# Filler products of layer 1, first half: four column tiles or the whole width of TensorE's array

## The chip, the cores and the metric

The kernel runs on one core of one Trainium2 chip. The metric is the device time of one execution in microseconds. Every measured program is run several times, and the median is compared.

## What is computed

Two cross-attention layers follow each other, for a batch of 4, all in float32. In layer 0, `x` (4, 1024, 512) goes through a layer norm and attends to `ctx_768` (4, 1024, 384) with 16 heads of 64. In layer 1, the result goes through an RMS norm and attends to the same context with 16 heads of 32. There the queries and keys are rotated by position and brought to unit length first. The core of layer 1, cut to what matters here:

```
q = (xn @ wq).reshape(B, T, 16, 32)
kv = (ctx @ wkv).reshape(B, T, 2, 16, 32);  k, v = kv[:, :, 0], kv[:, :, 1]
q, k = rotate(q, cos, sin), rotate(k, cos, sin)
q, k = q / norm(q), k / norm(k)
attn = softmax(einsum('bqhd,bkhd->bhqk', q, k) * sqrt(32))
out = x + einsum('bhqk,bkhd->bqhd', attn, v).reshape(B, T, 512) @ wout
```

## The kernel before, in words

The batch entries are worked through one after the other (loop at L739). For each, layer 0 runs over 8 pairs of heads (L746), and layer 1 over two halves of 8 heads each (L849). The change concerns layer 1.

**A step of layer 1.** One half is 32 steps: 4 blocks of 256 queries, 2 groups of 4 heads, and 4 pairs of key tiles (L885, L886). A step (`Attention1.step`, L590) puts this on the engines, in this order:

- *Scores*, L597: 8 matmuls, `s`, each with 32 rows and 128 columns of the array. Four heads lie in four row tiles of the array side by side, each 32x128. They fill two PSUM tiles of two banks each.
- Two exponentials on ScalarE, L607, from those PSUM tiles into `e`.
- *Products of the step before*, L636: 8 matmuls, `av`, each with 128 rows and 32 columns, so that four heads lie in four column tiles, each 128x32. After the last pair of key tiles, 8 more, L647, with a matrix of ones: the sums under the softmax. Those read `both`, which VectorE has added up.
- *Filler*, L611: `self.u.fill(us)` takes units from a queue and issues them until their assumed cost covers the share of this step.
- Additions on VectorE of the exponentials, L613 and L617, for the sums.

**The filler.** Whatever the attention of this half doesn't need yet is cut into units, each a function with a cost in microseconds written out by hand (`Units`, L54). `weave` (L94) sets them in order. In half 0 of layer 1 these are the projections of the remaining queries (`q[1]` to `q[3]`, `q1`), keys (`k1[2]`, `k1[3]`) and values (`vs`), 92 matmul units in all, each a product of a 128x128 block with 256 columns of weights (L490, L562). Between them lie 12 places with transposes by TensorE through an identity matrix: ten with 4 for a rotated query or key block (L519), and two, with 12 and 4, for the normalized rows (L253). In half 1 they are the projections of the next batch entry and the output product of this one.

**How wide a filler matmul is.** All filler products go through `matmul` (L153). It splits one product into `which["cols"]` instructions, each with a slice of the columns of the stationary matrix, so that each takes one column tile of the array:

```
w = P // which["cols"]
for j in range(which["cols"]):
    rr = slice(j * w, (j + 1) * w)
    nc.tensor.matmul(o[rr], lhsT[:, rr], rhs, start=start, stop=stop)
```

In layer 0, `cols` is 2 (L122, L899). L837 sets it to 4 for all of layer 1, the shape of `av`. The transposes don't go through it: they are always 128x128.

**After a projection.** When a query or key projection is complete, `rotate` (L494) follows. ScalarE squares it (L497), VectorE does five operations (L499 to L504), GpSimd does three (L506, L175, L510), and then TensorE transposes the result (L519) and ScalarE copies it out (L524). `post` (L163) issues this chain at once in layer 1. VectorE also divides (L654, L655) after each block.

**Order and due times.** The order on each engine is the order in which the program issues, since `manual_schedule` is on (L117). `marks` (L864) says up to which unit the queue must be worked off before steps 8, 16 and 24. PSUM has two score tiles of two banks (L120). One further bank is held by `av` in layer 1, and three banks rotate among the fillers (`bank`, L124).

Each float32 matmul stands in the trace as two pairs of records, LDWEIGHTS and MATMUL; a transpose stands as one. The text calls one MATMUL record of all tiles that work side by side a *pass*.

Of the kernel before, what the change touches and what calls it, by code (L numbers as in the profile page):

```python
# [93 lines left out]
def weave(chains, lag):  # L94

    res = []
    for i in range(len(chains) + lag):
        if i < len(chains):
            res += chains[i][0]
        if 0 < i <= len(chains):  # L100
            res += chains[i - 1][1]
        if i >= lag:
            res += chains[i - lag][2]
    return res
# [3 lines left out]
def xattn_kernel(ctx: ExitStack, tc: tile.TileContext, a: dict, out: bass.AP):  # L108
# [13 lines left out]
    which = {"n": 0, "from": 0, "cols": 2}  # L122
# [16 lines left out]
    cols = const.tile([P, 3, NQ], F32, name="cols")  # L139
# [152 lines left out]
    def add_units(xt, lhs, w, name, cs, then=None):  # L292

        n = len(cs)

        def one(t, i, pp=[None]):
            if i == 0:
                pp[0] = bank(f"{name}_{t}")
            matmul(pp[0], lhs(cs[i])[:, t * P : (t + 1) * P], w(cs[i]), i == 0, i == n - 1)
            if i == n - 1:  # L300
                nc.vector.tensor_add(xt[t], xt[t], pp[0])  # L301
                if then is not None:
                    then(t)

        return [[(0.86, lambda t=t, i=i: one(t, i)) for i in range(n)] for t in range(NT)]
# [250 lines left out]
    def value_chains(v, wv, ct, name):  # L556
        def one(t0, i, k, st={}):
            if i == 0 and k == 0:
                st["pp"] = bank(f"{name}_{t0}")
            t = t0 + i  # L560
            lhsT = ct[t // 4][:, k, (t % 4) * P : (t % 4 + 1) * P]
            matmul(st["pp"][:, i * FH : (i + 1) * FH], lhsT, wv[:, k, :], k == 0, k == NC_ - 1)  # L562
            if i == TH - 1 and k == NC_ - 1:
                pv = st["pp"].rearrange("p (t g d) -> p g t d", t=TH, g=2)
                for g in range(2):
                    nc.scalar.copy(v[g][:, t0 : t0 + TH, :], pv[:, g])

        return [
            ([(0.44, lambda t0=t0, i=i, k=k: one(t0, i, k)) for i in range(TH) for k in range(NC_)], [], [])
            for t0 in range(0, NT, TH)  # L570
        ]
# [89 lines left out]
    def wo_load(src, i, name):  # L661
        w = sb.tile([P, 2, DQ], F32, tag="wo", bufs=2, name=name)
        nc.sync.dma_start(w, src[i * 2 * P : (i + 1) * 2 * P, :].rearrange("(n p) m -> p n m", p=P))
        return w

    def flat(lists):
        return [u for lst in lists for u in lst]
# [71 lines left out]
    for b in range(B):  # L739
# [94 lines left out]
        work.add(norms[0]["turn"] + q[0][0] + k1[1][0] + k1[0][2] + flat(outs[4:]) + q[0][2])  # L834
        work.drain()

        which["from"], which["cols"] = 1, 4  # L837
        att1 = Attention1(b, work)
        o = [
            sb.tile([P, S], F32, tag="vals", bufs=4, name=f"o1_{b}_{g}") if g < 2 else None  # L840
# [7 lines left out]

        for half in range(2):  # L849
            n = 0  # L850
            if half == 0:
                vs = value_chains(att1.v1, wv1, ct, f"pv1_{b}_1")
                first = [q[1], (norms[1]["stats"], [], []), vs[0], (norms[1]["apply"], [], k1[1][2]), k1[2]]
                rest = [(norms[1]["turn"] + q[2][0], [], q[2][2]), k1[3], q[3], q1[0], vs[1], q1[1], q1[2]]
                rest += [q1[3], vs[2], vs[3]]
                chains = first + rest
                work.add(weave(chains, 2))
                def mark(c):

                    i = chains.index(c)  # L860
                    return sum(len(x[0]) for x in chains[: i + 3]) + sum(len(x[2]) for x in chains[: i + 1])

                base = work.done
                marks = {8: base + mark(q[1]), 16: base + mark(rest[0]), 24: base + mark(q[3])}  # L864
            else:
                for g in range(2, 4):
                    o[g] = sb.tile([P, S], F32, tag="vals", bufs=4, name=f"o1_{b}_{g}")
                wo1 = [wo_load(a["wout"], i, f"wo1_{b}_{i}") for i in range(2)]
                adds = add_units(xt, lambda n: o[n], lambda n: wo1[0][:, n % 2, :], f"po1_{b}_0", (0, 1))
                if b + 1 < B:  # L870
                    st, order = prepare_units(b + 1)
                    work.add(order(adds))
                else:
                    work.add(flat(adds))
            blocks = [(qb, g) for qb in range(S // WQ) for g in range(2)]
            final = b == B - 1 and half == 1
            if final:
                blocks.sort(key=lambda block: block[1])
                adds = [
                    add_units(  # L880
                        xt, lambda n: o[n], lambda n: wo1[1][:, n % 2, :], f"po1_{b}_{i}", (i,), store if i == 3 else None
                    )
                    for i in (2, 3)
                ]
            for qb, g in blocks:  # L885
                for kk in range(NT // 2):  # L886
                    if half == 0 and n in marks:
                        work.until(marks[n])
                    if final and n == 18:
                        work.add(flat(adds[0]))  # L890
                    if final and n in (22, 26, 30):
                        work.add(flat(adds[1][(n - 22) // 2 : (n - 18) // 2]))
                    att1.step(half, g, qb, kk, kT, qT, v, o[2 * half :], work.total() / (32 - n))
                    n += 1
            work.drain()
            kT, qT, v = kT1, qT1, att1.v1
# [48 lines left out]
```

## Time and profile before

| | |
|---|---|
| median of 3 runs | 2974.82 us (2970.41 to 2974.82) |
| the profiled execution, its own time | 2969.33 us |
| its span in the profile | 2967.1 us |
| granted TensorE clock | 0.999 |
| TensorE busy (matmul) | 2905.4 us, 98% |
| VectorE busy | 2230.9 us, 75% |
| ScalarE busy | 1430.4 us, 48% |
| half 0 of layer 1, the four batch entries | 508.3 to 638.8, 1242.7 to 1373.1, 1976.5 to 2106.9, 2711.8 to 2843.9 us |

The profile is of one execution; its own time is 5.5 us below the median of the runs. All times in the views are microseconds from the start of the span. A matmul's busy time overlaps with that of its neighbours, since they are pipelined and their ends are modelled. So distances from start to start are used below.

### The profile page before, as it was taken

The page shows a single profiled execution, that of the slowest core. Times are in us where ns is not written, and L with a number is a line of the kernel's source. Part 1 is how long each engine was busy: PE and PEld are TensorE (multiplying, and loading weights), DVE is VectorE, ACT ScalarE, POOL GpSimd, SP SyncE. Part 2 cuts the span into 40 slices and gives each one's busy share as a digit, 9 for nine tenths or more (in the row PEclk, how much of TensorE's full clock was granted, in tenths as well). Part 3 has the DMA queues.
Part 4 walks back from the last instruction along what each step waited for, and adds up shares of the span by engine and source line. Part 5 has one row for each costly group of instructions (what it writes and reads, how often), then busy time and mean ns, then how long its engine had stood idle before and what let it go on. Part 6 is the DMA issues. An engine that isn't in the chain of part 4 may idle for free.

```text
span 2967.1 us, 66793 instructions
## 1 busy us (share of the span) xinstructions
PE 2905.4 (98%) x27880; PEld 1454.7 (49%) x27880; DVE 2230.9 (75%) x2824; ACT 1430.4 (48%) x2265; POOL 417.2 (14%) x392
## 2 busy tenths in 40 slices
PE   8999999999999999999999999999999999999998
PEld 4544445555544444555544444455455444445544
DVE  4777795877777779587777777958767777785777
ACT  3444443666544444466644444446664443444664
POOL 0010022420000002232000000224100000023310
PEclk9999999999999999999999999999999999999999
DMA  5787674010388867301048777730105978772000
GB/s 146 173 198 181 158 178 111 21 35 25 80 205 192 186 159 179 91 22 35 25 100 214 182 182 171 165 79 22 35 25 120 211 177 186 166 171 62 2 2 30
DMA packets 177549, 348.88 MB, mean 118 GB/s; under 512 B 37600, under 2 KB 93152, under 8 KB 177248
## 3 DMA queue, kind: packets, MB, share of 16 engines
q1 hardware_dynamic: 175056, 343.43, 48.9%
q8 instruction: 220, 3.60, 0.5%
q10 hardware_dynamic: 2192, 1.19, 0.1%
q14 instruction: 81, 0.66, 0.1%
HBM read 67.64 MB, written 8.39 MB: 26 GB/s over the span
## 4 chain that ended last, share of the span: by engine, by line
PE 85%; DVE 7%; DMA 2%; ACT 2%; SPq 1%; issue 1%; POOL 1%; DVEq 0%; ACTq 0%
PE s L372 16%; PE av L449 14%; PE po L158 11%; PE pv L158 8%; PE s L597 7%; PE pqT L158 7%; PE av L636 6%; PE pkT L158 5%; PE q_p L158 3%; PE av L647 2%; PE k_p L158 2%; DVE both L613 2%; PE rT L440 1%; DVE both L617 1%; SPq L407 1%
## 5 line engine op out<-in xcount | busy, mean ns | idle before, releaser
L396 ACT ACTIVATE e<-s,m 128x1024 f32<-128x1024 f32 x512 | 566.1, 1110 | 666.3 <-DVE m L395 625.8
L395 DVE TENSOR_REDUCE m<-s 128x1 f32<-128x1024 f32 x512 | 602.7, 1219 | 314.0 <-PE s L372 314.0
L607 ACT ACTIVATE e<-s 128x1024 f32<-128x1024 f32 x512 | 496.7, 1022 | 312.4 <-PE s L597 297.3
L401 DVE STREAM_TRANSPOSE e<-e 128x1024 f32<-128x1024 f32 x512 | 606.7, 1223 | 47.6 <-ACT e L396 44.7
L372 PE MATMUL s<-qk 64*128 64x512 f32 x2048 | 521.3, 615 | 5.4 <-ACT e L396 4.7
L449 PE MATMUL av<-eT,v 128*64 128x256 f32 x4096 | 465.2, 380 | 7.3 <-DMA eT<-e 3.7
L613 DVE TENSOR_TENSOR both<-e 128x512 f32<-128x512 f32 x512 | 342.1, 700 | 125.0 <-ACT e L607 89.8
L449 PEld LDWEIGHTS av<-eT,v 128*64 128x64 f32 x4096 | 295.1, 137 | 186.2 <-issue 48.4
L372 PEld LDWEIGHTS s<-qk 64*128 64x128 f32 x2048 | 182.4, 186 | 269.2 <-issue 193.3
L597 PE MATMUL s<-q,k 32*128 32x256 f32 x4096 | 305.1, 401 | 5.8 <-ACT q L524 2.7
L597 PEld LDWEIGHTS s<-q,k 32*128 32x128 f32 x4096 | 191.2, 184 | 149.2 <-ACT e L607 72.0
L158 PE MATMUL po<-wo,vals 128*64 128x512 f32 x1024 | 239.7, 599 | 3.0 <-ACT v L130 3.0
L158 PE MATMUL pqT<-hT,w 128*64 128x512 f32 (+1 forms) x1216 | 241.4, 598 | 0.7 <-ACT hT L255 0.7
L441 ACT COPY vals<-rT 128x256 f32<-128x256 f32 x128 | 47.8, 373 | 323.7 <-PE rT L440 323.7
L301 DVE TENSOR_TENSOR x<-x,po 128x512 f32<-128x512 f32 x200 | 134.0, 678 | 83.0 <-PE po L158 82.7
L158 PEld LDWEIGHTS pv<-w,cT 128*64 128x64 f32 (+1 forms) x3648 | 168.5, 128 | 34.3 <-issue 31.2
L158 PE MATMUL pv<-w,cT 128*64 128x128 f32 (+1 forms) x3648 | 183.4, 274 | 0.0
L158 PE MATMUL pkT<-cT,w 128*64 128x512 f32 (+1 forms) x912 | 182.0, 601 | 0.9 <-ACT cT L130 0.9
L617 DVE TENSOR_TENSOR both<-both 128x1024 f32<-128x1024 f32 x128 | 159.7, 1248 | 4.4
L636 PE MATMUL av<-e,v 128*32 128x256 f32 x2048 | 137.1, 385 | 0.0
L636 PE MATMUL av<-e,rest 128*32 128x256 f32 x2048 | 137.0, 385 | 0.0
L158 PE MATMUL q_p<-wq,hT 128*32 128x256 f32 (+1 forms) x1920 | 131.2, 380 | 0.0
(461 smaller groups left out, 2482.0 us busy)
## 6 DMA issues: line engine op xcount, KB each, us to landing
eT<-e SPq DMA_DIRECT2D x2048, 128.0 KB, 2.4
xr<-in_x_dram SPq DMA_DIRECT2D x32, 256.0 KB, 4.1
x<-in_x_dram SPq DMA_DIRECT2D x32, 256.0 KB, 3.7
wo<-in_Wo_dram SPq DMA_DIRECT2D x16, 512.0 KB, 4.2
out_dram<-x SPq DMA_DIRECT2D x32, 256.0 KB, 2.6
w<-in_Wq_dram SPq DMA_DIRECT2D x31, 256.0 KB, 4.0
c<-in_ctx_dram SPq DMA_DIRECT2D x32, 192.0 KB, 3.8
wkv<-in_wkv_dram SPq DMA_DIRECT2D x16, 384.0 KB, 3.2
```

The source lines that it names most:

```text
L158: nc.tensor.matmul(o[rr], lhsT[:, rr], rhs, start=start, stop=stop)
L301: nc.vector.tensor_add(xt[t], xt[t], pp[0])
L372: nc.tensor.matmul(sc[j][:, kb * 512 : (kb + 1) * 512], pr["qT"][r[j], i * P : (i + 1) * P], pr["kT"][r[j], kb * 512 : (kb + 1) * 512], st ...
L395: nc.vector.tensor_reduce(m[:, j : j + 1], sc[j], AX.X, ALU.max, negate=True)
L396: nc.scalar.activation(e[j], sc[j].rearrange("p (g s) -> p g s", g=4), AF.Exp, bias=m[:, j : j + 1], accum_out=l[:, j : j + 1])
L401: nc.vector.transpose(e[j], e[j])
L449: nc.tensor.matmul(av[r[j], :W].rearrange("p (t a i) -> p t a i", t=BQ, a=4), pr["v"][:, k, r[j]], eT[:, j, :, :, k * 32 : (k + 1) * 32], ...
L597: nc.tensor.matmul(sc[j // 2][:, j % 2, c, :], kT[rr, g, k * P : (k + 1) * P], qT[rr, g, qb * WQ : (qb + 1) * WQ], start=True, stop=True,)
L607: nc.scalar.activation(e, sc[u], AF.Exp, scale=float(np.sqrt(np.float32(HD1))))
L613: nc.vector.tensor_add(self.both[:, kk, 2 * u : 2 * u + 2, :], es[u][:, :, 0, :], es[u][:, :, 1, :])
L617: nc.vector.tensor_add(self.both[:, 0], self.both[:, 0], self.both[:, kk])
L636: nc.tensor.matmul(self.av[rr, 0, :], v[g][:, 2 * kk + c, rr], es[j // 2][:, j % 2, c, :], start=first and c == 0, stop=end and c == 1,)
```

## The change

`cols` is no longer set once for layer 1, but at the start of each half: 1 in half 0, 4 in half 1. With 1, `matmul` issues one instruction with all 128 columns in place of four with 32 each. The 92 filler products of half 0 are then 92 instructions for each batch entry, in place of 368. What is computed, the order of the units, the steps into which they fall, and every other instruction stay the same.

```
-        which["from"], which["cols"] = 1, 4
+        which["from"] = 1
         att1 = Attention1(b, work)
...
         for half in range(2):
             n = 0
+            which["cols"] = (1, 4)[half]
             if half == 0:
```

More of the change, by code (lines that the diff above doesn't have):

```diff
@@ L835, in xattn_kernel @@
         work.drain()
-        which["from"], which["cols"] = 1, 4
+        which["from"] = 1
         att1 = Attention1(b, work)
@@ L850, in xattn_kernel @@
             n = 0
+            which["cols"] = (1, 4)[half]
             if half == 0:
```

## The prediction

> **What bounds the kernel now.** I read the busy shares first, then the chain that ended last, then the stage that changes.
>
> ```profile
> PE 2905.4 (98%) x27880; PEld 1454.7 (49%) x27880; DVE 2230.9 (75%) x2824; ACT 1430.4 (48%) x2265; POOL 417.2 (14%) x392
> ...
> PE 85%; DVE 7%; DMA 2%; ACT 2%; SPq 1%; issue 1%; POOL 1%; DVEq 0%; ACTq 0%
> ```
>
> TensorE is busy for 98% and makes 85% of the chain. By stretches (columns: busy us and instructions of PE, PEld, DVE, ACT, POOL), half 0 and then half 1 of layer 1 of the first batch entry:
>
> ```profile
> 508.30:638.80 130.50, 124.41 (x1916) 69.38 (x1916) 102.99 (x143) 82.33 (x109) 47.53 (x30) 1.00 0.06 17
> 638.80:770.50 131.70, 131.42 (x1979) 69.68 (x1978) 92.73 (x129) 82.55 (x100) 3.75 (x4) 1.00 0.12 35
> ```
>
> Half 0 is the one stage where PE stands idle for some microseconds (6.1 of 130.5), and DVE is at 79%. So extra PE time there is paid, except what falls into those waits. The steps themselves (start, length, records; PE timeline):
>
> ```profile
> 508.31 1.15 PE L597 MATMUL s<-q,k 32*128 32x256 f32 x16 [0.68 <-ACT q L524]
> 509.39 1.93 PE L158 MATMUL q_p<-wq,hT 128*32 128x256 f32 x32
> 511.25 1.36 PE L597 MATMUL s<-q,k 32*128 32x256 f32 x16
> 512.55 1.07 PE L636 MATMUL av<-e,v 128*32 128x256 f32 x16
> 513.44 1.48 PE L158 MATMUL q_p<-wq,hT 128*32 128x256 f32 x24
> 514.85 1.15 PE L597 MATMUL s<-q,k 32*128 32x256 f32 x16
> ...
> 526.33 0.66 PE L519 MATMUL q_t<-ident,rot 128*128 128x128 f32 x4 [0.57 <-POOL rot L510]
> 526.92 1.07 PE L158 MATMUL k_p<-wkv,cT 128*32 128x256 f32 x16
> 527.92 1.15 PE L597 MATMUL s<-q,k 32*128 32x256 f32 x16
> ```
>
> A pass of four tiles with 256 columns takes 216 ns from start to start (single records in the trace). Two column tiles: 216 too; transposes: 109. From these and the line starts I take the price of each change of shape, as an exit part (paid by the last pass of the old shape) and an entry part (paid by the first of the new):
> - `av` after `s`: 512.55 to 513.44 = 889 ns, 4 passes are 864: entry into 128x32 costs 24.
> - filler after `av`, then `s`: 513.44 to 514.85 = 1409, 6 passes are 1296: nothing at entry, exit from 128x32 costs 114.
> - transposes, then filler: 526.33 to 526.92 = 587 against 4 x 109 = 436: 56 at entry, 94 at exit.
> - `s`, then `av`: 1075 (508.31 to 509.39 rounds it), against 864: 104 at entry of 32x128, 108 at exit.
>
> These numbers give back every undisturbed run of PE in the half within 2 ns.
>
> [...] The trace agrees: 94 to 114 ns at each change, none between `av` and a filler of the same shape. [...] The entry costs agree: 24 (128x32), 51 (128x64, layer 0), 104 (32x128). Transposes, 56, are faster than that. [...] The trace agrees for 128x128 transposes: 109 a pass, load included.
>
> **The change, part by part.** The built order of PE shows the same steps, with 92 filler instructions in place of 368 per batch entry.
>
> *Passes.* 92 units x 2 passes stay 184 passes. No full-width float32 product is in this trace. I take 216 ns, as with two and four tiles[...]. Gain or loss zero; bounds 196 (below) and 216 + 105 = 321 if the load were not hidden.
>
> *Changes of shape.* Full width enters at about 104 (by the columns; between 0[...] and 104; transposes show 56) and exits at 94 as a single tile (transposes). Between transposes and full-width products the shape is the same: I take 0; the upper bound is a full change, 94 + 104 or 94 + 56. The 32 steps of a half 0 fall into these kinds:
> - 19 with filler only after `av` or the sums: a new change, 114 + 104, less 20 at the exit: +198.
> - 4 with transposes, then filler: change saved, 94 + 24, and 20 at the exit: -138.
> - 5 with filler, then transposes: +218, less 114 + 56: +48.
> - 3 with transposes between filler: +218 less (114 + 56) less (94 + 24) less 20: -90.
> - step 0, with no `av`: 104 for 24, 94 for 114: +60.
>
> Sum: 19 x 198 - 4 x 138 + 5 x 48 - 3 x 90 + 60 = 3240 ns per batch entry, 13.0 us in all.
>
> *What the waits take back.* The prices above sum to 120.3 us for a half 0 that takes 130.5, so PE waits about 10 us in it for something else (6.1 shows as idle; in the rest some of the tiles wait while others run). If that hangs on an event before the delay, the wait shrinks by the delay. The largest:
>
> ```profile
> 622.63 0.61 PE L647 MATMUL av<-both,ones 128*32 128x256 f32 x8
> 625.47 1.01 PE L647 MATMUL av<-both,ones 128*32 128x256 f32 x6 [2.22 <-DVE both L613]
> ```
>
> DVE has been busy without a break since
>
> ```profile
> 610.57 0.69 DVE L499 TENSOR_TENSOR rot<-q_p,cos 128x512 f32<-128x512 f32 x1 [2.65 <-ACT rot L497]
> ```
>
> which ACT's L497 (609.94) released, and that the end of the filler of step 24. So all delay from steps 25 to 27 vanishes here. I go through the half with the delay D in ns:
> - step 0: +60, gone in step 1, whose scores wait 218 for an exponential. Step 1: D = 198.
> - steps 2 and 3: their 396 vanish in step 4 (waits of 734 in its scores and 635 before its transposes; ACT, DVE and GpSimd run in one chain from the scores of step 2). Rest of step 4, -138: 60.
> - step 5: 258; step 6's transposes wait 1.67 on DVE, in the same chain: 198. Steps 7, 8: 258.
> - step 9's filler ends at 258 + 218 = 476 and starts the next DVE chain (549.16); the sums of step 12 wait 2.36 on it: 476, after its transposes 338.
> - step 13: 536; filler of step 14: 754, starting the chain of 570.26; sums of step 16: 754, then 952. Step 17: 862, 18: 1060, 19: 1108.
> - sums of step 20, wait 0.17, chain from the exponentials of step 17: 952, then 1150. Steps 21 to 23: 1456.
> - sums of step 24, wait 0.17, chain from step 22: 1348, its filler ends at 1566; sums of step 28: 1566, then 1764. Steps 29 to 31: 2058.
>
> So 2.06 us of the 3.24 remain; half 1 has PE waits of 0.6 us only, and passes it on. The last entry's half 1 waits more (15 us), but for ScalarE and VectorE that follow its own scores, which come later by the same D. 4 x 2.06 = 8.2 us. On the profiled execution, 2969.33 + 8.2 = 2977.6; the median of runs stands 5.5 higher, so I state 2974.82 + 8.2 = 2983.0. Covers that could go: the order on ACT, DVE, POOL and the queues does not change, and no DMA waits for a filler of this half closely (share 0.06).
>
> **Rivals.** About 0.2% (6 us) is what a measurement can tell from no change.
> - *No relief from the waits* (D is carried whole): 13.0, 2987.8. For: anchors such as ACT's L497 at 609.94 wait for the filler's end themselves. Against: DVE's unbroken runs before the waits.
> - *Transposes and products don't share a mode*: 7 exits from transposes into products at 198, and 8 the other way at 150, are 2.6 us per entry; 8.2 + 10.3 = 18.5, less some relief: about 2990. For: a transpose has one pass and a faster load. Against: same rows and columns.
> - [...]entry of 0 in place of 104 makes a plain step +94; the same walk ends at 0.7 us per entry: 2.8, 2977.6, no visible change. With 56 it ends at 1.4: 5.6. Against: all three loads above show at entry.
> - *Full-width loads are not hidden at all*: 184 x 105 ns = 19.3 us per entry, 77 in all, 3060. Against: the transposes' 109.
> - *Faster*: the four tiles of a pass start 7 ns apart, 20 in all, and 196 lie from the last to the next. If a single tile saved those 20, the passes of the filler would take 196: 184 x 20 = 3.7 us per entry against 2.06, or 6.5 us faster, 2968.3. It decides from a pass below 205 ns on (2.06 us / 184 = 11 ns). Against: transposes and 32-column tiles with 128 columns both take 109, so the stagger costs nothing.
>
> **How the numbers follow.** Chances: my forecast 0.49 (its own range 2979 to 2988), no relief 0.15, no shared mode 0.12, [...] 0.13, loads exposed 0.04, faster 0.07. Predicted: 2983. The range, 2976 to 2996, takes in the hidden load below, and no relief and the unshared mode above; it leaves out the exposed loads and the faster case. Slower by over 0.2%: 0.42 of my 0.49, and 0.31: 0.73. Within: 0.07 and 0.13: 0.20. Faster: 0.07.
>
> **What would show it.** In the profile after: a filler pass of 216; 1409 + 104 - 20 for 3 units after `av` (about 1493), with `av` before it at 864 + 24 + 114 = 1002 in place of 889; transposes to filler at 109, not 203; half 0 at 132.5 us in place of 130.5, half 1 unchanged; the PE waits for `both` (3.8 us) shorter. Wrong if `av` stays at 889, or if transposes still pay at each end.

## The result, and the profile after

The changed kernel takes 2979.14 us (median of 13 runs, 2976.32 to 2985.89) against 2970.41 us for the kernel before (13 runs in all with the three shown first, 2966.13 to 2974.97). The ratio is 1.003, with a 95% interval from 1.0022 to 1.0038: slower by 8.7 us, and by 6.5 to 11.3 within the interval. The forecast was 8.2. The profiled execution took 2979.14 us, with a span of 2976.8.

On the page after, matmul busy time is up by 11.1 us, with 2208 records fewer:

```profile
PE 2916.5 (98%) x25672; PEld 1492.5 (50%) x25672; DVE 2231.1 (75%) x2824; ACT 1432.6 (48%) x2265; POOL 416.8 (14%) x392
```

Busy times by stretch after, half 0 and half 1 of the first batch entry, columns as before:

```profile
508.90:641.30 132.40, 126.86 (x1360) 78.74 (x1360) 103.03 (x143) 82.35 (x109) 47.53 (x30) 1.00 0.05 16
641.30:773.30 132.00, 131.71 (x1979) 69.73 (x1978) 92.82 (x129) 82.81 (x101) 3.74 (x4) 1.00 0.12 35
```

Half 0 went from 130.5 to 132.4 us. Half 1 hardly moved. In half 0, DVE, ACT and POOL do the same work in the same time as before. The same steps on PE as in the prediction, now after the change:

```profile
508.93 1.15 PE L597 MATMUL s<-q,k 32*128 32x256 f32 x16 [0.68 <-ACT q L524]
510.00 1.99 PE L158 MATMUL q_p<-wq,hT 128*128 128x256 f32 x8
511.93 1.30 PE L597 MATMUL s<-q,k 32*128 32x256 f32 x16
513.16 1.07 PE L636 MATMUL av<-e,v 128*32 128x256 f32 x16
514.16 1.56 PE L158 MATMUL q_p<-wq,hT 128*128 128x256 f32 x6
515.65 1.15 PE L597 MATMUL s<-q,k 32*128 32x256 f32 x16
...
527.14 0.66 PE L519 MATMUL q_t<-ident,rot 128*128 128x128 f32 x4 [0.57 <-POOL rot L510]
527.64 1.03 PE L158 MATMUL k_p<-wkv,cT 128*128 128x256 f32 x4
528.60 1.15 PE L597 MATMUL s<-q,k 32*128 32x256 f32 x16
```

`av` to filler now takes 513.16 to 514.16, 1.00 us, where it was 0.89: the exit from four column tiles is paid there. The 6 passes of the filler take 514.16 to 515.65, 1.49 us, where it was 1.41. Before, they paid nothing at entry and 0.11 at the exit from four column tiles; now they pay a load of 128 columns at entry (0.10) and an exit of 0.09. The four transposes take 0.50 to the next product (527.14 to 527.64), where it was 0.59: nothing is paid at their exit. These nine lines hold both signs that the prediction asked for.

Measured exactly, from the start of the first score matmul to that of the next half, the four halves 0 take 130.46, 130.46, 130.46 and 132.09 us before, and 132.41 each after. The 132.09 holds 1.6 us more in steps 28 and 29 than the other three. The trace shows why: the granted TensorE clock (the third figure from the end) falls to about half there, for 3.4 us:

```profile
2830.00:2833.00 3.00, 3.00 (x28) 1.36 (x24) 2.85 (x4) 0.59 (x1) 2.92 (x2) 0.52 0.03 5
```

Such a stretch stands in other runs at other places, also where nothing was changed: after, from 1650.3 to 1653.7 us, in layer 0, at a clock of 0.50. Each half 0 in the traces of this document that is 1.4 to 1.6 us longer than its siblings holds one, and no other half 0 does. So the undisturbed 130.46 is what to compare with: the delay is 1.95 us per half 0, 7.8 in all. The halves 1 add 0.24, 0.30, -0.10 and 0.02. That makes 8.2 in this pair of profiles, beside 8.7 us between the medians. The distance of the two spans (9.7 us) is made up otherwise: it lacks the 1.6 us that the profile before lost to the clock, and holds 3.1 more in layer 0, which the change doesn't touch. From half 1 of one entry to half 0 of the next, layer 0 takes 472.2, 471.6 and 472.2 us before, and 473.1, 474.4 and 471.0 after; the 474.4 holds that stretch at half clock, and what else scatters there was not traced.

### The profile page after: what moved, and what is told of

Same layout as the page of the kernel before. It is cut to its first block, busy times and chain, and to the rows that moved or that the text cites. A ratio compares the mean times of both kernels' runs of the same rounds, so it can differ in the third digit from the quotient of the medians.

```text
span 2976.8 us, 62377 instructions
## 1 busy us (share of the span) xinstructions
PE 2916.5 (98%) x25672; PEld 1492.5 (50%) x25672; DVE 2231.1 (75%) x2824; ACT 1432.6 (48%) x2265; POOL 416.8 (14%) x392
## 4 chain that ended last, share of the span: by engine, by line
PE 83%; DVE 9%; DMA 2%; ACT 2%; SPq 1%; issue 1%; POOL 1%; DVEq 0%; ACTq 0%
PE s L372 15%; PE av L449 13%; PE po L158 10%; PE pv L158 8%; PE s L597 7%; PE pqT L158 7%; PE av L636 6%; PE pkT L158 5%; PE q_p L158 4%; PE av L647 2%; DVE both L613 2%; PE k_p L158 1%; PE rT L440 1%; DVE e L401 1%; DVE m L395 1%
## 5 line engine op out<-in xcount | busy, mean ns | idle before, releaser
L613 DVE TENSOR_TENSOR both<-e 128x512 f32<-128x512 f32 x512 | 342.7, 700 | 125.7 <-ACT e L607 90.0
L617 DVE TENSOR_TENSOR both<-both 128x1024 f32<-128x1024 f32 x128 | 159.7, 1248 | 4.4
L158 PE MATMUL q_p<-wq,hT 128*128 128x256 f32 (+1 forms) x576 | 132.6, 393 | 0.0
```

Source lines behind the costliest of these rows:

```text
L613: nc.vector.tensor_add(self.both[:, kk, 2 * u : 2 * u + 2, :], es[u][:, :, 0, :], es[u][:, :, 1, :])
L617: nc.vector.tensor_add(self.both[:, 0], self.both[:, 0], self.both[:, kk])
```

## The experiments

The theory was that of the prediction: filler after a product pays a change of the array's shape, transposes ahead of filler save one, and later waits in half 0, most of them on VectorE, take back a third of the sum. Rivals: the extra time belongs to half 0 rather than to the shape; the price grows with the width of an instruction; nothing is taken back, and the price was over-estimated.

### Full width in half 1 alone

The edit is against the changed kernel, as is the next one.

```
-            which["cols"] = (1, 4)[half]
+            which["cols"] = (4, 1)[half]
```

> The filler is full-width in half 1 alone, four tiles in half 0. If the delay is the price of changes of shape (218 ns after each product, 20 back at the exit, 118 saved after transposes), half 1 of the first three batch entries, which has 24 plain steps, 4 with transposes ahead of the filler and 3 with transposes behind it, gets longer by 24 x 198 - 4 x 138 + 3 x 48 + 336 = 4.7 us each, nearly all of it paid since TensorE waits for only 0.6 us there; the last entry's, with 9 steps without filler and 15 us of waits, by 2 to 4.7. In all 16 to 19 us slower than the kernel before. If instead the extra time in half 0 comes from something of that half (its VectorE chains, its transposes), half 1 gets longer by less than 2 us each.

Measured: 2990.49 us (4 runs), ratio 1.0068 (1.0054 to 1.0082), 20 us slower (16 to 24), where 16 to 19 were expected. Halves 0 stand at 130.4 again, but for one with a stretch at half clock. By stretches, half 1 of the first entry and of the last:

```profile
638.60:775.40 136.80, 136.53 (x1425) 73.69 (x1424) 92.92 (x129) 82.66 (x100) 3.74 (x4) 1.00 0.11 33
...
2858.20:2977.00 118.80, 113.22 (x1245) 53.71 (x1244) 92.65 (x121) 67.83 (x75) 0.00 (x0) 1.00 0.04 15
```

The four are longer by 5.1, 5.0, 4.4 and 3.3 us (the first 136.8 against 131.7, the last 119.2 against 115.8, from start to start), 17.8 in all; the rest up to 20 was not traced. By the prices of the prediction, passes and changes of shape in the first come to 131.06 us before and 135.74 here, the 4.68 expected. Of the other 0.4, 0.2 lie in the passes of 128 columns, which take 112 ns in place of 109, and 0.2 in waits. So the extra time is not something of half 0; that it goes by the shape and not by the width, the next two runs show. Where few transposes stand next to the filler and PE waits little, the same edit costs two and a half times as much (5.1 us against 1.95).

### Two column tiles in half 0

```
-            which["cols"] = (1, 4)[half]
+            which["cols"] = (2, 4)[half]
```

> The filler of half 0 stands in two column tiles of 64, a shape that fits neither the products (128x32) nor the transposes (128x128). Shape theory: entry after a product costs 114 + 51, and nothing is saved at the transposes, so half 0 gets longer by 19 x 151 + 4 x 13 + 5 x 151 + 3 x 164 = 4.2 us before the waits and by about 2.5 us after them: more than with full width (1.9), though a tile is half as wide. In all 9 to 11 us slower than before. Width theory (wider instructions overlap worse, so the price grows with the width): between four tiles and full width, about 1 us per half 0, 4 us in all.

Measured: 2981.57 us (4 runs), ratio 1.0042 (1.0027 to 1.0058), 11 us slower. The stretch of half 0, and one of its steps on PE:

```profile
508.70:641.50 132.80, 127.54 (x1544) 69.52 (x1544) 103.22 (x143) 82.51 (x109) 47.56 (x30) 1.00 0.05 16
```

```profile
512.97 1.07 PE L636 MATMUL av<-e,v 128*32 128x256 f32 x16
513.98 1.52 PE L158 MATMUL q_p<-wq,hT 128*64 128x256 f32 x12
515.42 1.15 PE L597 MATMUL s<-q,k 32*128 32x256 f32 x16
```

Half 0 takes 132.76 us, 2.30 more than before and 0.35 more than with full width. A single entry is cheaper than full width's (513.98 to 515.42, 1.44 us against 1.49), since the entry with 64 columns is 51 ns and not 104. But nothing is saved at the transposes: from the last of them to the filler it is 202 to 203 ns, as before, and not 109. The width theory, which puts it at 1 us, falls. The size was expected at 2.5 and is 2.3: the prices come to 4.2, and the waits take back 1.9. Four times 2.3 is 9.2 of the 11 us between the medians. How much else can lie between two profiles, one half 1 of this run shows: with the same instructions as before it is 3.8 us longer, for a wait of 1.8 us for rows of the context (`c<-in_ctx_dram`) and a stretch at half clock behind it.

### Full width only behind transposes

```
+    def turned():
+        if which["mix"]:
+            which["cols"] = 1
...
+            turned()
             nc.scalar.copy(dst[:, :, t0 * P : (t0 + TH) * P], pt.rearrange("p (g t) -> p g t", g=2))
...
+            which["cols"] = 4
             self.u.fill(us)
```

`turned()` also stands in the other two places with transposes, and `mix` is set in layer 1 alone.

> The filler stays in four column tiles, but units that follow transposes within a step of layer 1 are full-width up to the next product, in both halves. Shape theory: 7 places in half 0 save 94 + 24 + 20 = 138 ns each, of which the waits on VectorE leave about 0.28 us of 0.97; 4 places in half 1 save 0.55 us. In all 2 to 3.5 us faster than the kernel before, below what a median shows, but plain in the lengths of the halves: half 0 130.2 and half 1 131.1 us. If full width costs something by itself, both halves are longer than before.

Measured: 2971.44 us (13 runs), ratio 1.0005 (0.9996 to 1.0013): no difference that the medians can tell. The lengths of the halves tell more (first entry):

```profile
508.50:638.70 130.20, 123.72 (x1844) 71.13 (x1844) 102.98 (x143) 82.34 (x109) 47.49 (x30) 1.00 0.06 17
638.70:770.30 131.60, 131.32 (x1943) 70.19 (x1942) 92.72 (x129) 82.56 (x100) 3.75 (x4) 1.00 0.12 35
```

From start to start, half 0 of the first entry is 130.19, 0.27 us shorter than before, as expected to 0.01; so is that of the third, and the other two hold stretches at half clock. The prices alone gave 0.97; the waits are longer by the 0.70. Half 1 is 131.62, 0.08 shorter and not 0.55. At two of its four places the filler behind the transposes waits for ScalarE, which copies out what transposes made. It starts 316 and 505 ns after the last of them, as before (316 and 506), so no exit is saved, and the load of 128 columns is then added to its first pass (533 ns against 454). One of the two, before and here (the lines of the kernel have moved by 4 to 8):

```profile
712.60 1.06 PE L158 MATMUL pqT<-hT,w 128*32 128x512 f32 x8 [0.23 <-ACT hT L255]
```

```profile
712.35 1.12 PE L158 MATMUL pqT<-hT,w 128*128 128x512 f32 x2 [0.23 <-ACT hT L261]
```

So the full width costs nothing where filler follows the transposes without a wait, but in half 0 most of the time that it saves on PE is waited away, and in half 1 two places of four save nothing. If all entries went like the first, that would make 1.3 us, where 2 to 3.5 were expected; it is too little to call this a better kernel. A step of half 0 with the saved change:

```profile
526.49 0.66 PE L525 MATMUL q_t<-ident,rot 128*128 128x128 f32 x4 [0.56 <-POOL rot L516]
526.98 1.03 PE L158 MATMUL k_p<-wkv,cT 128*128 128x256 f32 x4
527.94 1.15 PE L604 MATMUL s<-q,k 32*128 32x256 f32 x16
```

Transposes 0.49 and filler 0.96, against 0.59 and 1.00: the 138 ns.

### The waits taken away

Two kernels, alike but for the filler's width in half 0. Both take work from VectorE there by leaving out the additions of L617, so that the sums under the softmax lack terms:

```
-            if 0 < kk < NT // 2 - 1:
+            if 0 < kk < NT // 2 - 1 and half == 1:
                 nc.vector.tensor_add(self.both[:, 0], self.both[:, 0], self.both[:, kk])
```

> Leaves out the additions of L617 in half 0 (16 per half of 1.23 us on VectorE), so the sums under the softmax miss terms; four tiles. Partner of the next run, which differs from it only in the width of the filler. TensorE's waits in half 0 should fall from 10.2 to about 4 us (those on ScalarE and GpSimd stay), half 0 to about 124 us. If VectorE's chains were not what TensorE waits for, half 0 stays at 130.5.

> The same left out, filler of half 0 full-width. Theory that VectorE's waits took back a third of the price: without them half 0 is longer than its partner by 2.6 to 3.0 us, not by the 1.9 measured with them (only the waits of steps 1, 4 and 6 on ScalarE and GpSimd still take back some). If nothing is taken back by those waits and the price itself was over-estimated: 1.9 again.

Measured, one run each: 2953.24 us with four tiles, 2969.07 with full width. The times of single runs scatter too much for a few us to be read from them; the halves 0 don't. With four tiles:

```profile
508.90:636.30 127.40, 123.00 (x1916) 69.22 (x1916) 82.64 (x127) 82.10 (x109) 46.70 (x30) 1.00 0.06 17
```

With full width:

```profile
509.30:639.50 130.20, 125.80 (x1360) 78.61 (x1360) 82.64 (x127) 82.08 (x109) 46.94 (x30) 1.00 0.06 16
```

From start to start 127.38 against 130.19, in all four entries: 2.80 us, inside 2.6 to 3.0, where the same edit costs 1.95 with VectorE's full work. So waits on VectorE do take back time, 0.85 us per half, and the price was not over-estimated. The other 0.44 of the 3.24 are still taken back here, nearly all at steps 1 and 4, where the scores wait for ScalarE.

What missed is the length with four tiles: 124 was expected, 127.4 came. PE still waits 7.1 us, though DVE works 20 us less. The sums of step 12 wait 2.3 us, nearly as before (2.36). Why, DVE's timelines show, before:

```profile
556.67 0.68 DVE L499 TENSOR_TENSOR rot<-k_p,cos 128x512 f32<-128x512 f32 x1
```

and in the four-tile kernel, whose half starts 0.57 us later:

```profile
557.06 0.69 DVE L499 TENSOR_TENSOR rot<-k_p,cos 128x512 f32<-128x512 f32 x1 [2.37 <-ACT rot L497]
...
559.65 2.51 DVE L613 TENSOR_TENSOR both<-e 128x512 f32<-128x512 f32 x4
```

DVE now stands idle for 2.37 us, until ACT's L497 has squared the key projection of step 11, whose end L497 awaits. So the rotation starts only 0.18 us earlier in the half than before. The additions that the sums need (L613) are queued on DVE behind it. The wait is nearly as long as before, but hangs on the end of the filler of the step just before, and takes back nothing any more: 2.32 us with four tiles, 2.28 with full width.

## Why the prediction was right

**Passes.** Assumed at 216 ns for full width; the 456 passes that stand between two others of the filler take 215 or 216, and those right behind transposes 218. The load of 128 columns stands in a record of 190 ns that starts 2 ns after a pass does, and passes of 256 columns still follow each other at 216. So the rivals of exposed loads (about an entry of 104 more for each pass) and of shorter passes are out.

**Changes of shape.** The first pass after `av` comes 329 ns after the last of `av`: the exit from 128x32 is 113. The second comes 320 later: 104 of entry, as the prediction took it from the entry of 32x128. From the last pass to the scores it is 309: the exit is 93. From transposes into products 109, from products into transposes 216: no price in either direction, so those two count as one shape. (The prediction's line for entry and exit of the scores, 508.31 to 509.39, is followed by filler and not by `av`; both have the shape 128x32, and the price is the same.) The rivals of an entry of 0 (chance 0.13) and of an unshared mode fall by these four numbers; the trace before had no full-width products. That the entry goes with the weight load, the load records show: behind a change of shape, the loads of the second pass start 28 ns after those of the first with 32 columns, 55 with 64 and 108 with 128, where the entries are 24, 51 and 104. With transposes it is 59 for an entry of 56.

**The sum.** Put on all 520 passes of half 0 of the first entry, in their order, the prices come to 120.29 us before and 123.53 after: 3.24 more, the value that was worked out from 32 steps. The distances from pass to pass bear them out: before 493 of the 520, and after 501, lie within 15 ns of their price, and together these miss it by 0.04 and 0.05 us. The other distances hold the waits, 10.2 us before and 8.9 after.

**What the waits take back.** Forecast 1.18 of the 3.24, measured 1.30: 0.45 at steps 1 and 4, where the scores wait for ScalarE, and 0.85 at the waits on VectorE, in step 6 and at the sums of steps 12 to 28. The walk holds step by step: the delay of the starts is 0.20 us at step 7 (forecast 0.198), 0.46 at step 10 (0.456), 0.31 at step 13 (0.338), 1.07 at step 21 (1.150), 1.65 at step 29 (1.764). Its largest slip is one term: of the delay at the end of the filler of step 14, all 754 ns were passed to the chain of VectorE. But ACT's L497 (569.63 before) came right behind the exponentials and had some room, so step 17 starts 0.87 us later and not 0.95. The wait of the sums of step 28, after:

```profile
625.01 0.61 PE L647 MATMUL av<-both,ones 128*32 128x256 f32 x8
627.53 1.23 PE L647 MATMUL av<-both,ones 128*32 128x256 f32 x8 [1.91 <-DVE both L613]
```

It shows 1.91 us idle in place of 2.22, and VectorE's chain, after, starts 2.07 later than before, with the end of the filler of step 24:

```profile
612.64 0.69 DVE L499 TENSOR_TENSOR rot<-q_p,cos 128x512 f32<-128x512 f32 x1 [2.84 <-ACT rot L497]
```

Of those 2.07, 0.61 are the later start of the whole half, so the chain carries 1.46 us. That this relief is real, and not an over-estimated price, the pair without L617 shows, with 2.80 us in place of 1.95.

**The rest.** Half 1 was to pass the delay on unchanged; it added 0.1 us on average, which was not traced. The forecast of 2983.0 stands 3.9 above the measured median because it started from 2974.82, the median of the three runs shown, and thirteen gave 2970.41. The difference, 8.2 against 8.7, is inside the interval. That the pair of profiles gives 8.2 too is luck in part: the halves 0 came to 7.8, and the halves 1 happened to add the 0.4 that was missing.

## What to carry to other kernels

Here the width of a float32 product of 256 columns cost nothing by itself (216 ns a pass with one, two or four column tiles), but a change of shape between neighbours did: an exit of 93 to 114 ns and an entry of 24, 51 or 104 ns for 32, 64 or 128 columns of weights (56 for transposes). So count neighbours, and ask what filler stands beside, products or transposes. A delay on the busiest engine is paid only as far as no later wait hangs on an event before it (here 1.95 of 3.24 us): walk through the step list with the delay, wait by wait. Do the same for a gain, of which 0.27 of 0.97 us was left.

## What the runs showed that was not expected

- With 128 columns of weights, passes of 128 columns took hardly longer: in half 1 at full width the value projections of layer 0 take 112 ns a pass, against 109 with 32 columns a tile.
- Taking 20 us of work from VectorE shortened a half by 3.1 us only: at step 12 its chain could start no sooner than ScalarE's L497 let it, and VectorE stood idle for 2.37 us instead.
- Where filler behind transposes waits for ScalarE anyway, full width saves nothing there, and the load of 128 columns is paid (two places in half 1, first pass 533 ns against 454).
